# A two-layer kernel with a selective scan on one core: instruction order fixed in slots with three streams, and pairs of state products summed before their transpose

## The chip, the core and the metric

The kernel runs on one core of a Trainium2 chip. A core has TensorE (PE, matrix multiplies; its weight loads are shown apart as PEld), VectorE (DVE), ScalarE (ACT), GpSimd (POOL) and SyncE (SP, which here only issues DMAs). Each engine works through its own queue in order, and semaphores hold an instruction until its inputs are there and its buffer is free. The metric is device time in microseconds for one execution.

## What is computed

A sequence of 2048 rows of 512 float32 values goes through two layers. All arithmetic is float32.

```python
# layer 0
h = layernorm(x) * (1 + ca) + sa
x = x + ga * (h @ (block-masked W).T + bias)
h = layernorm(x) * (1 + cb) + sb
x = x + gb * lora_ffn(h)              # silu(gate) * up, hidden width 1376
# layer 1
h = layernorm(x) * (1 + ca) + sa
x, gate = split(h @ W_in.T)           # 1024 channels each
x = silu(causal_conv4(x))
ts, B, C = split(x @ W_x.T)           # 32, 16, 16 columns, each RMS-normed
dt = softplus(ts @ W_dt.T + b_dt)
for t in sequence:                    # 16 states n for each of 1024 channels
    state[n] = state[n] * exp(dt * A[n]) + dt * u * B[n]
    y = sum_n state[n] * C[n]
y = (y + x * D) * silu(gate)
x = x + ga * (y @ W_out.T)
h = layernorm(x) * (1 + cb) + sb
x = x + gb * (h @ base.T + 2 * top2_lora_experts(h))
```

The vectors sa, ca, ga and so on come from two small products with modulation weights, once for each layer.

## The kernel before

**Tiling.** The 2048 rows are cut into 8 chunks (`c`) of 256. The scan of a chunk runs in 32 steps: two halves of the channels (`a`, four tiles of 128 channels each) times 16 states (`n`). One such step is called a slot here; there are 256, and the loop over `ALL` makes them. Channels lie on the partitions, time along the free dimension, so a slot works on tiles of 128 x 1024 (four channel tiles of 256 time steps).

**One slot.** SP brings the rows B and C of state `n`, spread over all partitions (`bcn`, line 473). ACT makes the decays `da` two slots ahead (line 469). VectorE multiplies `bx = dtu * B` into PSUM (line 687), adds the carry of the chunk before into the first column of each tile (line 689) and runs the recurrence as one scan, `hb = scan(da, bx)` (line 690). ACT copies the last column out as the next carry (`states`, line 695). GpSimd multiplies `hc = hb * C` in two pieces of 128 x 512 (line 697). In the slot after, TensorE transposes the eight 128 x 128 blocks of `hc` and adds them in PSUM to `ys` (`add_t`, line 450): the sum over the 16 states is made there, by 16 x 8 transposes for each half. `da`, `hb` and `hc` have three buffers each, taken in turn; `bx` has one.

**Work beside the scan.** Everything else is written as generators, which issue a piece of work and yield its cost in us of TensorE time. `first_layer(c)` is layer 0 of a chunk: two norms with transposes (`norm_t`, lines 148 to 177), the masked product (line 286), gate and up projections (line 304) and the down projection (line 323). `beside(c)` holds, in this order, `out_proj(c-1)` (lines 509 to 525), `gate_proj(c)` (line 489), in the first chunk `late_setup` (scaled weights of layer 1), then `front(c+1)` (norm, input projection line 374, convolution line 394, B, C and dt rows lines 405 to 416) and `experts(c-1)` (lines 562 to 625). After the transposes of a slot the loop draws pieces worth 2.4 us from `beside` and 1.8 us from the first layers. At slot 10 of a second half it issues all that is left of `beside`; at slot 12 of each half it issues `steps` (dt, line 433) and `inputs` (`dtu`, line 439) of the next half.

**Order.** The order of writing is not the order on the engines. The tile framework's scheduler sorts the instructions of all engines by priority and by its own estimate of when each is ready, and places the waits.

**Buffers and queues.** Weights that don't stay in SBUF pass through 12 buffers `ws` of 256 KB, loaded on SP; temporaries have 5 buffers `tmp`; `bcn` has 6, fetched 4 slots ahead. PSUM has 4 banks for products, 2 for `ys`, 2 for `bx`. The weights of the experts' base product (`w_base`, 1 MB) stay in SBUF. `late_setup` loads its weights on ACT's queue.

**Before and after the loop.** The modulation, the masked weights, `first_layer(0)` and `front(0)` run ahead of the loop; the last `out_proj` and `experts` run behind it.

Of the kernel before, what the change touches and what calls it, by code (L numbers as in the profile page):

```python
# [23 lines left out]
R = 16  # L24
# [13 lines left out]
def mamba_block_kernel(  # L38
# [14 lines left out]
    small = ctx.enter_context(tc.tile_pool(name="small", bufs=2))  # L53
    xpool = ctx.enter_context(tc.tile_pool(name="x", bufs=5 * NM))
    wsp = ctx.enter_context(tc.tile_pool(name="ws", bufs=12))
    tpool = ctx.enter_context(tc.tile_pool(name="tmp", bufs=5))
    hpool = ctx.enter_context(tc.tile_pool(name="hT", bufs=1))
    hid = ctx.enter_context(tc.tile_pool(name="hid", bufs=6))
    upool = ctx.enter_context(tc.tile_pool(name="u", bufs=6))
    zpool = ctx.enter_context(tc.tile_pool(name="z", bufs=2 * NM))  # L60
    bcp = ctx.enter_context(tc.tile_pool(name="bc", bufs=6))
# [3 lines left out]
    ps_b = ctx.enter_context(tc.tile_pool(name="ps_b", bufs=1, space=PSUM))  # L65

# [22 lines left out]

    xs = {}  # L90
# [11 lines left out]
    da, hc = by_half("da", 3), by_half("hc", 3)  # L102
    hb_w = [keep.tile([P, FF], FP, name=f"hb{i}") for i in range(3)]
    hb = [t[:, : TH * TC].rearrange("p (t n) -> p t n", t=TH) for t in hb_w]
# [43 lines left out]
    def norm_t(xt, scale, shift, tag):  # L148
        st = small.tile([P, NM, 6], FP, tag="st", name="st")
        mv = small.tile([P, NM, 2], FP, tag="mv", name="mv")  # L150
        for m in range(NM):
            V.bn_stats(st[:, m, :], xt[m])  # L152
            V.bn_aggr(mv[:, m, :], st[:, m, :])  # L153
        rs = small.tile([P, NM], FP, tag="rs", name="rs")
        G.tensor_scalar(rs, mv[:, :, 1], LN_EPS, None, ALU.add)
        G.tensor_tensor(rs, rs, power, ALU.pow)
        off = small.tile([P, NM], FP, tag="off", name="off")
        V.scalar_tensor_tensor(off, mv[:, :, 0], -1.0, rs, ALU.mult, ALU.mult)
        xn = []
        for m in range(NM):  # L160
            t = tmp()
            S.activation(t, xt[m], AF.Identity, bias=off[:, m : m + 1], scale=rs[:, m : m + 1])  # L162
            xn.append(t)
        h = hpool.tile([P, NK, TC], FP, tag=tag, bufs=2 if tag == "h0" else 1, name="h")
        for k2 in range(NK // 2):
            ps = halves(bank())
            for i in range(2):
                k = 2 * k2 + i
                for m in range(NM):
                    T.transpose(ps[:, i, m * P : (m + 1) * P], xn[m][:, k * P : (k + 1) * P], ident)  # L170
            for i in range(2):
                k = 2 * k2 + i
                S.activation(  # L173
                    h[:, k, :], ps[:, i, :], AF.Identity, bias=shift[:, k : k + 1], scale=scale[:, k : k + 1]
                )
            yield 0.5
        return h
# [46 lines left out]
    ranks = [t.rearrange("p t n -> p (t n)")[:R, :DM] for t in hc]  # L224
    wides = [t[:R, :] for t in hb_w]
    for dst, src in zip(ranks + wides, (gate_a, up_a, down_bt, gate_bt, up_bt, down_a)):
        nc.gpsimd.dma_start(out=dst, in_=src)
    ga_r, ua_r, db_r = ranks
    gb_w, ub_w, da_w = wides
# [4 lines left out]
    down_s = dram.tile([len(HT), P, DM], FP, name="down_s")  # L234
    wout_s = dram.tile([ND, P, DM], FP, name="wout_s")

    def wide_tile(src, scratch, a_r, b_w, j, first):
# [8 lines left out]
        for k in range(NK):  # L246
            T.matmul(
                ps[:, k * n : (k + 1) * n], lhsT=a_r[:, k * P : (k + 1) * P], rhs=b_w[:, h0 : h0 + n],
                start=True, stop=True,
            )  # L250
# [4 lines left out]
    def down_tile(j, first):  # L255
# [8 lines left out]
        T.matmul(ps[:n, :], lhsT=da_w[:, h0 : h0 + n], rhs=db_r, start=True, stop=True)  # L264
# [5 lines left out]

    def first_layer(c):
        xt = xs[c]
        if c + 1 < NC:
            load(c + 1)
        h = yield from norm_t(xt, ca, sa, "h0")
        acc = [bank() for m in range(NM)]
# [13 lines left out]
        for m in range(NM):  # L290
            V.tensor_tensor(xt[m], xt[m], acc[m], ALU.add)
        h = yield from norm_t(xt, cb, sb, "h0")
        hidden = []
        product = None
        for j0 in range(0, len(HT), 2):
# [4 lines left out]
            pg, pu = halves(bank()), halves(bank())  # L300
            for w2, ps in ((ws_g, pg), (ws_u, pu)):
# [6 lines left out]
                yield 1.75 * len(js)  # L308
            ht = hid.tile([P, 2, TC], FP, tag="hid", name="hidden")
            up = halves(tmp())  # L310
            view = (slice(0, n), slice(0, len(js)))
            S.activation(ht[view], pg[view], AF.Silu)  # L312
            S.copy(up[view], pu[view])  # L313
            if product is not None:
                V.tensor_tensor(*product, ALU.mult)  # L315
            product = ht[view], ht[view], up[view]
            hidden.append(ht)
        V.tensor_tensor(*product, ALU.mult)
# [9 lines left out]
        for m in range(NM):  # L328
            V.tensor_tensor(xt[m], xt[m], acc[m], ALU.add)
        done.add(c)  # L330

    for _ in first_layer(0):
        pass
# [24 lines left out]
    def front(c):  # L358
        nonlocal halo
        h = yield from norm_t(xs[c], ca1, sa1, "h1")  # L360
        new_halo = keep.tile([P, ND, KC - 1], FP, name=f"halo{c % 2}", tag=f"halo{c % 2}")
        us = []
        for t2 in range(ND // 2):
            ps = halves(bank())
            xp = small.tile([P, 2, TC + KC - 1], FP, tag="xp", name="xp")
            for i in range(2):
# [6 lines left out]
                for k in range(NK):  # L373
# [3 lines left out]
                    )  # L377
                yield 1.75
            if halo is None:
                G.memset(xp[:, :, : KC - 1], 0.0)  # L380
            else:
                G.tensor_copy(xp[:, :, : KC - 1], halo[:, 2 * t2 : 2 * t2 + 2, :])
            S.copy(xp[:, :, KC - 1 :], ps)
            if c + 1 < NC:
                G.tensor_copy(new_halo[:, 2 * t2 : 2 * t2 + 2, :], xp[:, :, TC:])
            acc = halves(tmp())
            for i in range(2):
                t = 2 * t2 + i
                S.activation(  # L389
                    acc[:, i, :], xp[:, i, KC - 1 :], AF.Identity,  # L390
                    bias=ch[:, t, C_B : C_B + 1], scale=ch[:, t, C_W + KC - 1 : C_W + KC],
                )
                for j in range(KC - 1):
                    V.scalar_tensor_tensor(  # L394
                        acc[:, i, :], xp[:, i, j : j + TC], ch[:, t, C_W + j : C_W + j + 1],
                        acc[:, i, :], ALU.mult, ALU.add,
                    )
            u = upool.tile([P, 2, TC], FP, tag="u", name="u")
            S.activation(u, acc, AF.Silu)
            us.append(u)  # L400
        halo = new_halo

# [5 lines left out]
        yield 3.5  # L408
        sq = tmp()
        S.activation(sq[:64, :TC], ps[:64, :TC], AF.Square)  # L410
        ps2 = bank()
        T.matmul(ps2[:64, :TC], lhsT=rms_m, rhs=sq[:64, :TC], start=True, stop=True)
        S.activation(sq[:64, TC:], ps2[:64, :TC], AF.Sqrt, bias=eps_rms[:64, :])
        V.reciprocal(sq[:64, :TC], sq[:64, TC:])
# [3 lines left out]
        nc.sync.dma_start(out=bc.rearrange("a n t -> (a n) t"), in_=ssm[RDT:, :])  # L418
        fed[c] = (h, us, ssm, bc)
        yield 0.5  # L420

    bx = ps_b.tile([P, TH, TC], FP, name="bx")

    def steps(c, a):
        us, ssm = fed[c][1:3]
        for i in range(TH):
            t = a * TH + i
            ps = bank()
            T.matmul(
                ps[:, :TC], lhsT=wdt[:, t * P : (t + 1) * P], rhs=ssm[:RDT, :], start=True, stop=True  # L430
            )
            dst, src, b_dt = dt[a][:, i, :], ps[:, :TC], ch[:, t, C_DT : C_DT + 1]
            S.activation(dst, src, AF.Softplus, bias=b_dt)  # L433
# [21 lines left out]
    def skip(c, a):  # L455
        us = fed[c][1]
        for t2 in range(TH // 2):
            ud = halves(tmp())
# [21 lines left out]
    def gate_proj(c):  # L480
        h = fed[c][0]
        zs[c] = [zpool.tile([P, DM], FP, tag="z", name="z") for _ in range(2 * NM)]
        for a in range(2):
            acc = [bank() for m in range(NM)]
# [8 lines left out]
            for m in range(NM):  # L493
                S.activation(zs[c][2 * m + a], acc[m], AF.Silu)

    def gating(c, a):
        for m in range(NM):
            z = zs[c][2 * m + a]
            V.tensor_tensor(z, z, ys[m], ALU.mult)

    def out_proj(c):
        xt = xs[c]
        acc = [bank() for m in range(NM)]
        for t2 in range(ND // 2):
            ps = halves(bank())
# [7 lines left out]
            g = halves(tmp())  # L513
            S.copy(g, ps)  # L514
            for i in range(2):
                t = 2 * t2 + i
                w = ws()
                nc.sync.dma_start(out=w, in_=wout_s[t])
                for m in range(NM):
                    T.matmul(  # L520
                        acc[m], lhsT=g[:, i, m * P : (m + 1) * P], rhs=w, start=t == 0, stop=t == ND - 1
                    )
                yield 2.0
        for m in range(NM):
            V.tensor_tensor(xt[m], xt[m], acc[m], ALU.add)  # L525
# [270 lines left out]
```

## Time and profile before

| What | Value |
|---|---|
| median of three runs | 1911.51 us (1905.35 to 1913.41) |
| the profiled execution, its own time | 1914.97 us |
| span of its trace (first to last instruction) | 1913.2 us |
| first scan starts, last one ends (the loop) | 242.8 us, 1869.8 us |
| mean granted TensorE clock | 0.881 |
| ACT busy | 1003.0 us (52%) |
| GpSimd busy | 879.3 us (46%) |
| DMA traffic | 233.42 MB, 122 GB/s over the span |

The trace is of one execution. Its page lists the busy time of each engine, and then groups of equal instructions with their count, busy time, mean duration, and the idle time of their engine just before them with what ended it. Busy time of TensorE is modelled: neighbouring matmuls overlap, so a busy TensorE is not one at its peak. The granted clock is the share of full speed that TensorE was allowed in a stretch. The durations of GpSimd contain the time in which an instruction has begun but is held up.

### The profile page before, as it was taken

The numbers are of one execution on the slowest core, as the hardware profiler recorded it, in microseconds if no ns is written. First come the engines' busy times: TensorE is split into PE (matmuls) and PEld (weight loads), VectorE is DVE, ScalarE is ACT, GpSimd is POOL, SyncE is SP. The second block draws the span as 40 slices with busy tenths as digits, with TensorE's granted clock in tenths as the row PEclk, the third lists the DMA queues.
The fourth block names the chain that finished last, engine by engine and source line by source line (L and its number), as shares of the span: only waits on it lengthen the run. The fifth ranks groups of instructions, "written<-read, shape, count | busy, mean of one in ns | idle before, by whom it ended". The sixth has DMA issues, their size and how long they took to land. (4 is left out here: it accounts for less than half of the span.)

```text
span 1913.2 us, 20659 instructions
## 1 busy us (share of the span) xinstructions
PE 1577.2 (82%) x6568; PEld 1075.1 (56%) x6568; DVE 1385.8 (72%) x1563; ACT 1003.0 (52%) x2093; POOL 879.3 (46%) x721
## 2 busy tenths in 40 slices
PE   4899779878897689879888879878888979767666
PEld 4685648545565466556546645555546655644433
DVE  2222395796877877887878886897678896989992
ACT  0100463557655565666565665575466765565631
POOL 0133072463553454544544554455344555547671
PEclk9689779988998899989898989898898989878877
DMA  8454345563554245534464345433353345423320
GB/s 248 147 159 165 102 124 172 149 192 99 143 149 104 85 125 151 128 100 122 130 153 103 95 114 142 118 98 119 115 149 110 95 124 147 121 51 98 72 51 11
DMA packets 192367, 233.42 MB, mean 122 GB/s; under 512 B 17009, under 2 KB 128497, under 8 KB 192258
## 3 DMA queue, kind: packets, MB, share of 16 engines
q1 hardware_dynamic: 176800, 200.13, 38.6%
q10 hardware_dynamic: 10434, 15.81, 2.5%
q0 software_dynamic: 5024, 16.16, 2.3%
q8 instruction: 52, 0.85, 0.2%
q14 instruction: 57, 0.47, 0.1%
HBM read 215.99 MB, written 16.06 MB: 121 GB/s over the span
## 5 line engine op out<-in xcount | busy, mean ns | idle before, releaser
L697 POOL TENSOR_TENSOR hc<-hb,bcn 128x512 f32<-128x512 f32 x512 | 777.1, 1538 | 642.1 <-PE y L450 469.7
L690 DVE TENSOR_TENSOR_SCAN hb<-da,bx 128x1024 f32<-128x1024 f32 x256 | 584.7, 2284 | 117.4 <-POOL hc L697 91.9
L469 ACT ACTIVATE da<-dt,neg_a 128x255 f32<-128x255 f32 x1024 | 440.9, 497 | 65.3 <-DVE hb L690 48.7
L304 PE MATMUL ps<-h,ws 128*128 128x256 f32 (+1 forms) x1408 | 344.6, 400 | 26.5 <-ACT hidden L312 18.3
L687 DVE TENSOR_TENSOR bx<-dtu,bcn 128x1024 f32<-128x1024 f32 x256 | 356.2, 1392 | 11.3 <-DMA bcn<-bc 5.0
L450 PE MATMUL y<-ident,hc 128*128 128x128 f32 x2048 | 303.2, 293 | 49.7 <-POOL hc L697 49.0
L304 PEld LDWEIGHTS ps<-h,ws 128*128 128x128 f32 (+1 forms) x1408 | 276.2, 200 | 99.2 <-issue 22.1
L450 PEld LDWEIGHTS y<-ident,hc 128*128 128x128 f32 x2048 | 256.1, 151 | 134.3 <-POOL hc L697 73.3
L695 ACT COPY states<-hb 128x4 f32<-128x4 f32 x224 | 43.5, 196 | 367.5 <-DVE hb L690 353.8
L520 PE MATMUL ps<-ws,tmp 128*128 128x512 f32 x256 | 151.8, 739 | 63.4 <-ACT tmp L514 63.3
L323 PE MATMUL ps<-ws,hidden 128*128 128x512 f32 (+1 forms) x352 | 161.6, 599 | 0.8 <-DVE ws L265 0.8
L394 DVE SCALAR_TENSOR_TENSOR tmp<-xp,ch,tmp 128x256 f32<-128x256 f32 x192 | 115.5, 649 | 19.9 <-ACT tmp L389 19.1
L520 PEld LDWEIGHTS ps<-ws,tmp 128*128 128x128 f32 x256 | 57.2, 238 | 129.5 <-ACT tmp L514 70.5
L374 PE MATMUL ps<-h,ws 128*128 128x256 f32 x512 | 125.1, 395 | 0.7 <-ACT h L173 0.7
L489 PE MATMUL ps<-ws,h 128*128 128x512 f32 x256 | 120.5, 602 | 2.6 <-ACT hidden L312 2.6
L374 PEld LDWEIGHTS ps<-h,ws 128*128 128x128 f32 x512 | 98.8, 200 | 16.5 <-ACT h L173 3.8
L323 PEld LDWEIGHTS ps<-ws,hidden 128*128 128x128 f32 (+1 forms) x352 | 64.0, 192 | 69.8 <-issue 63.1
L315 DVE TENSOR_TENSOR hidden<-hidden,tmp 128x512 f32<-128x512 f32 x40 | 38.9, 971 | 81.1 <-ACT tmp L313 81.1
L170 PE MATMUL ps<-ident,tmp 128*128 128x128 f32 x256 | 51.8, 343 | 52.6 <-ACT tmp L162 52.6
L162 ACT ACTIVATE tmp<-x,off,rs 128x512 f32<-128x512 f32 x64 | 48.9, 806 | 87.8 <-DVE mv L153 46.0
L469 ACT ACT_TABLE_LOAD x71 | 91.1, 1283 | 1.1
L170 PEld LDWEIGHTS ps<-ident,tmp 128*128 128x128 f32 x256 | 39.5, 178 | 72.6 <-ACT tmp L162 60.9
(140 smaller groups left out, 1575.7 us busy)
## 6 DMA issues: line engine op xcount, KB each, us to landing
bcn<-bc SPq DMA_DIRECT2D x256, 256.0 KB, 5.1
ws<-gate_s SPq DMA_DIRECT2D x70, 256.0 KB, 4.6
ws<-up_s SPq DMA_DIRECT2D x70, 256.0 KB, 4.7
ws<-down_s SPq DMA_DIRECT2D x70, 256.0 KB, 5.2
ws<-win_x_t_dram SPq DMA_DIRECT2D x64, 256.0 KB, 5.7
ws<-win_z_t_dram SPq DMA_DIRECT2D x64, 256.0 KB, 3.2
ws<-wout_s SPq DMA_DIRECT2D x64, 256.0 KB, 4.3
ws<-wmod_dram ACTq DMA_DIRECT2D x36, 256.0 KB, 3.2
```

The costliest lines, as they stand in the source:

```text
L170: T.transpose(ps[:, i, m * P : (m + 1) * P], xn[m][:, k * P : (k + 1) * P], ident)
L304: T.matmul(ps[:n, i, :], lhsT=w3[:, k, :], rhs=h[:, k, :], stop=k == NK - 1, **start_only(4 * i + k),)
L323: T.matmul(acc[m], lhsT=hidden[j // 2][:n, j % 2, m * P : (m + 1) * P], rhs=w[:n, :], start=j == 0, stop=j == len(HT) - 1,)
L374: T.matmul(ps[:, i, :], lhsT=w3[:, k, :], rhs=h[:, k, :], stop=k == NK - 1, **start_only(4 * i + k),)
L394: V.scalar_tensor_tensor(acc[:, i, :], xp[:, i, j : j + TC], ch[:, t, C_W + j : C_W + j + 1], acc[:, i, :], ALU.mult, ALU.add,)
L450: T.matmul(ys[m][:, i * P : (i + 1) * P], lhsT=src[:, m * P : (m + 1) * P], rhs=ident, start=first and i == 0, stop=last, is_transpose=Tru ...
L469: S.activation(da[q % 3][:, i, 1:], dt[a][:, i, 1:], AF.Exp, scale=neg_a[:, t, n : n + 1])
L489: T.matmul(acc[m], lhsT=h[:, k, m * P : (m + 1) * P], rhs=w, start=k == 0, stop=k == NK - 1)
L520: T.matmul(acc[m], lhsT=g[:, i, m * P : (m + 1) * P], rhs=w, start=t == 0, stop=t == ND - 1)
L687: V.tensor_tensor(bx, dtu[a], bcn[:, 0:1, :].to_broadcast([P, TH, TC]), ALU.mult)
L690: V.tensor_tensor_scan(h.rearrange("p t n -> p (t n)"), d.rearrange("p t n -> p (t n)"), bx.rearrange("p t n -> p (t n)"), 0.0, ALU.mult, ...
L697: G.tensor_tensor(hcn[:, i : i + 2, :], h[:, i : i + 2, :], bcn[:, 1:2, :].to_broadcast([P, 2, TC]), ALU.mult)
```

## The change

1. **Fixed order.** From the loop on, the order of writing is the order on PE, DVE, ACT and GpSimd (`manual_schedule`); SP is left to the framework. The writer keeps a clock of its own (`tick`), in us of TensorE work. An evacuation, an activation or a VectorE step that follows a product is written when that clock has moved on by a stated delay (`later`), and generators yield `WAIT` times.
2. **Three streams.** The first layers, `beside` (now with `steps` and `inputs` of both halves in it) and `experts` are three streams with shares 1.8, 2.0 and 0.4. A slot draws 2.3 us of work twice (4.0 us twice in the first half of chunk 0, where the first layers have share 6.0). A stream is passed over while it waits, while its PSUM banks or temporaries are taken (`NEED`), or while another stream holds the pair of accumulating banks (`HOLD`, `FREE`). The forced completion at slot 10 goes. First layers may run up to two chunks ahead of the scan.
3. **Pairs.** `hc` has four buffers. In an even slot, between the two draws, VectorE adds the `hc` of the two slots before, `due[0] += due[1]`, 128 x 1024 in SBUF; in the odd slot after it, TensorE transposes the sum: 8 transposes for two states in place of 16.
4. **Small moves.** The norm's `off` goes from VectorE to two GpSimd instructions; the halo copies of the convolution go from GpSimd to ACT; the copy of `states` is written 3.0 us later; `late_setup` loads on SP; the base weights of the experts are scaled once, written to DRAM (`base_s`) and loaded again in each chunk through `ws`, and their product follows the choice of the experts; `out_proj` makes all its transposes ahead of its products; `steps` puts two products in a bank. Three DMAs more split the wide rank weights ahead of the first layer. `ws` has 11 buffers, `tmp` 7, `bcn` 5 (fetched 3 slots ahead); `ud`, `g` and the norm's columns have pools of their own.

The loop afterwards, and the code around it that sets the order:

```diff
-    da, hc = by_half("da", 3), by_half("hc", 3)
+    da, hb, hc = by_half("da", 3), by_half("hb", 3), by_half("hc", 4)
...
         G.tensor_scalar(rs, mv[:, :, 1], LN_EPS, None, ALU.add)
+        G.tensor_scalar(off, mv[:, :, 0], -1.0, None, ALU.mult)
         G.tensor_tensor(rs, rs, power, ALU.pow)
-        V.scalar_tensor_tensor(off, mv[:, :, 0], -1.0, rs, ALU.mult, ALU.mult)
+        G.tensor_tensor(off, off, rs, ALU.mult)
+        yield WAIT, 5.0
+        yield NEED, 0, NM
...
+    def pump(streams, budget):
+        total = sum(st.share for st in streams if not st.ended) or 1.0
+        for st in streams:
+            if not st.ended:
+                st.credit = min(st.credit + budget * st.share / total, 12.0)
+        while budget > 0:
+            best = max((st for st in streams if ready(st)), key=lambda st: st.credit, default=None)
+            if best is None:
+                tick(min(budget, 0.5))
+                budget -= 0.5
+            else:
+                budget -= step(best)
+        return budget
...
     def beside(c):
+        yield from steps(c, 1)
         if c > 0:
             yield from out_proj(c - 1)
         yield from gate_proj(c)
...
             yield from front(c + 1)
-        if c > 0:
-            yield from experts(c - 1)
+            yield from steps(c + 1, 0)
...
     for q, (c, a, n) in enumerate(ALL):
...
+        first.share = 1.8 if c > 0 or a == 1 else 6.0
+        streams = [first, second, third]
+        budget = 2.3 if c > 0 or a == 1 else 4.0
+        while q + AHEAD < len(ALL) and ALL[q + AHEAD][:2] not in stepped:
+            pump(streams, 0.5)
+        h, d, hcn, bcn = hb[q % 3], da[q % 3], hc[q % 4], bcs.pop(0)
...
-        if n == NS - 6 and a == 1:
-            while not finished:
-                cost = next(second, "end")
...
-        if n == NS - 4 and nxt[0] < NC:
-            steps(*nxt)
-            inputs(*nxt)
         if q + 2 < len(ALL):
             decays(q + 2)
         V.tensor_tensor(bx, dtu[a], bcn[:, 0:1, :].to_broadcast([P, TH, TC]), ALU.mult)
...
         for i in range(0, TH, 2):
             G.tensor_tensor(
                 hcn[:, i : i + 2, :], h[:, i : i + 2, :], bcn[:, 1:2, :].to_broadcast([P, 2, TC]), ALU.mult
             )
+        if c + 1 < NC:
+            later(3.0, lambda a=a, n=n, h=h: S.copy(states[a][:, :, n], h[:, :, TC - 1]))
+        over = pump(streams, over + budget)
+        if n == 2 and q > NS:
+            gating(*ALL[q - 3][:2])
+        if n == 3:
             skip(c, a)
-        if due is not None:
+        due.append((hcn, n))
+        if n % 2 == 0 and len(due) > 2:
+            V.tensor_tensor(due[0][0], due[0][0], due[1][0], ALU.add)
+        if n % 2 == 1 and len(due) > 2:
+            src, at = due[0][0], due[1][1]
+            due = due[2:]
             for i in range(TH):
-                add_t(i, due[:, i, :], False, n == 0)
-        due = hcn
...
+                add_t(i, src[:, i, :], False, at == NS - 1)
+            tick(1.1)
+        over = pump(streams, over + budget)
```

## Prediction

> **What bounds the kernel now.** I read the busy line of the page first, then the loop by stretches, then who waits for whom, then single slots.
>
> ```profile
> PE 1577.2 (82%) x6568; PEld 1075.1 (56%) x6568; DVE 1385.8 (72%) x1563; ACT 1003.0 (52%) x2093; POOL 879.3 (46%) x721
> ```
>
> No engine is full. TensorE comes first, but its 82% is modelled time. The starts of neighbouring matmuls in the trace lie 0.109 us apart for a 128-column transpose, 0.216 for 256 columns and 0.43 for 512 (medians). By these the loop's matmuls need 1196 us at full clock, and 1196/0.89 = 1344 at the clock granted there, of a loop of 1627. The stretches (columns: us, then PE, PEld, DVE, ACT, POOL busy with counts, clock, DMA share, GB/s) are the whole loop, two halves of chunk 3, and the two halves of chunk 7:
>
> ```profile
> 242.80:1869.80 1627.00, 1346.19 (x5714) 911.65 (x5713) 1312.29 (x1407) 953.93 (x2007) 831.81 (x636) 0.89 0.43 118
> 892.60:983.60 91.00, 77.64 (x318) 50.23 (x317) 72.62 (x61) 57.90 (x125) 49.25 (x32) 0.92 0.50 132
> 983.60:1101.00 117.40, 99.17 (x445) 70.53 (x444) 98.34 (x129) 70.61 (x148) 53.91 (x51) 0.90 0.41 110
> 1724.90:1798.60 73.70, 59.58 (x248) 37.22 (x249) 69.20 (x67) 45.87 (x96) 53.83 (x34) 0.86 0.39 100
> 1798.60:1869.80 71.20, 40.70 (x170) 24.10 (x168) 68.85 (x65) 28.05 (x68) 50.35 (x32) 0.75 0.21 45
> ```
>
> VectorE is busy 1312 of 1627 us, so it idles 315. Where the side work runs out (chunk 7) it is busy 94% and 97%: there it is the bound. In the chunks before, VectorE and TensorE wait for each other in turn:
>
> ```profile
> POOL hc L697 <- PE y L450: 469.7, 132, 19.3
> DVE hb L690 <- POOL hc L697: 91.9, 39, 7.2
> DVE hidden L315 <- ACT tmp L313: 81.1, 19, 9.7
> DVE dtu L439 <- ACT dt L433: 58.4, 19, 6.0
> ```
>
> The first two are one chain: late transposes keep `hc`, so GpSimd is late, keeps `hb`, and the scan waits. The others are work issued in lumps, before its inputs are there.
>
> **The pair sum: what it takes away.** 2048 transposes of `hc` become 1024: 1024 x 0.109 = 112 us of TensorE, 125 at clock 0.89. TensorE's need falls from 1344 to 1219 us, far below VectorE's. So I count this gain as nothing by itself; it makes TensorE punctual, which works through the idle time below.
>
> **What it adds.** 128 adds of 128 x 1024 on VectorE, both inputs in SBUF. No such instruction is in the trace; the nearest is `bx`, also 128 x 1024 from two SBUF tiles, which goes to PSUM: shortest 1199 ns, median 1233. An instruction starts some 80 ns before its neighbour ends, so I take 1.15 us: 128 x 1.15 = 147 us.
>
> The price is not only that. In slot 1172 to 1181 and in a run of six convolution steps GpSimd and VectorE overlap:
>
> ```profile
> 1177.35 3.48 POOL L697 TENSOR_TENSOR hc<-hb,bcn 128x512 f32<-128x512 f32 x2 [2.30 <-PE y L450]
> 1177.40 2.30 DVE L687 TENSOR_TENSOR bx<-dtu,bcn 128x1024 f32<-128x1024 f32 x1
> ...
> 428.70 4.47 DVE L394 SCALAR_TENSOR_TENSOR tmp<-xp,ch,tmp 128x256 f32<-128x256 f32 x6
> 428.92 2.78 POOL L697 TENSOR_TENSOR hc<-hb,bcn 128x512 f32<-128x512 f32 x2 [0.57 <-PE ps L170]
> ```
>
> `bx` takes 2.30 instead of 1.23 because one `hc` piece (1.27 median) began first; six steps of 0.47 take 4.47 because two pieces slip in between, each after the step that held it up. The scan, whose `bx` is in PSUM, never moves (2244 to 2289 ns), nor does gating with `y` in PSUM (660 to 687). So VectorE instructions with both inputs in SBUF and GpSimd's `hc` exclude each other. The new add stands just where GpSimd has `hc` of the scan before it to do: if the add begins right after the scan, the first piece follows it and the next `bx` waits for that piece; if a stream's step comes first, the add itself waits.
>
> Call the wait per add b. Below: 0, the lone `bx` (no gain is possible, since the add only takes the tiles). Above: two pieces, 2 x 1.27 = 2.5; that can't hold for most adds, since the second piece falls under the next scan, which lets it run, so one piece, 1.27, is the end that I carry into the range. `bx` shows 1392 - 1233 = 0.16 on average, `dtu` (both in SBUF, not placed behind a scan, 665 shortest, 1168 mean in the loop) 0.50, a full block 1.13 (`dtu`'s longest, 1802, less 665). I take 0.8, halfway from `dtu` to the full block, because of the place: 128 x 0.8 = 102 us.
>
> The Trainium skill, "SBUF — State Buffer", section "Who interferes with whom", says that a VectorE instruction with two SBUF inputs and a GpSimd instruction that reads SBUF lock each other out for the whole instruction, whoever issues first. It speaks against the change more strongly than my 0.8: a whole piece for each add would be 128 x 1.27 = 163 us in place of 102, and the forecast 65 us later.
>
> **Norm.** `off` leaves VectorE: 27 x 0.46 = 12 us in the loop. GpSimd gets two small instructions more for each norm (0.3 us, as line 155) behind `hc`; it is 51% busy, and `off` was waited for 24.3 us in all, now inside a stated 5 us wait. Gain 12 us.
>
> **The order.** The loop's VectorE sum becomes 1312 - 12 + 147 + 102 = 1549 us. What idle time stays? The forced completion, `steps` and `inputs` in a lump, and `hc` freed late go. By the writer's clock a chunk offers 32 x 4.6 + 16 x 1.1 = 165 us and its side work is 134 (69 first layer, 53 `beside`, 12 experts), so the streams fit without overrun. TensorE has slack, ACT (954 of 1627) too. I take the 6% of chunk 7's first half, which still carries `out_proj` and `gate_proj`: 1549/0.94 = 1648. Bounds: 3% (the last half) gives 1597, 10% gives 1721.
>
> **Chunk 0.** Its first half now offers 16 x 8.0 + 8 x 0.87 = 135 us of TensorE work at full clock, 153 at 0.88, against 105.7 us for that half and 84 us of such work in it before. VectorE needs there only 71 + 8 x 1.95 = 87, 95 to 100 with the front brought forward. TensorE is the bound for some 50 us; part returns, since work brought forward (up to 51 us of TensorE, some 10 us of VectorE, and an emptier second half) is missing later. I charge 30; from 0 (the streams wait too, and idle ticks pass quickly) to 50.
>
> **The small moves.** Halo copies: 52 x 0.2 = 10 us to ACT, hidden by its slack; uncovered they would add at most these 10. Table loads (139 in the loop, 1.28 each) may rise when activations of three streams mix; ten more per chunk are 100 us, making ACT 1060 of 1650: hidden too. Base weights: 32 loads of 256 KB, 8.4 of 233 MB at a DMA share of 0.43: hidden; the row for such loads shows 8.0 us of waits (`ws` of `attn_s`, 128 products), so 8 uncovered. `late_setup` on SP passes the `bcn` loads: VectorE waited 5.0 us for `bcn` in all, ACT 5.5 behind its own weight loads; these trade, 0, from -5 to +21 (the longest wait for such a weight). Prefetch of `bcn` (6 less 4 slots, now 5 less 3) is tied to the same `hc` two slots back: 0. The three DMAs on POOL at the start cost some 0.6 us each beside a TensorE that is full there: 0.
>
> At the end, `experts` now makes the base product after the choice. Before, its 7.34 us ran from 1894.97 beside VectorE's 3.7 us of choosing. Now it starts after the transposes: 4 us.
>
> **Sum.** Loop 1648 + 30 - 1627 = +51, end +4: 1914.97 + 55 = 1970 for an execution like the profiled one, which is 3.5 over the median. Forecast 1966 us.
>
> **Rivals.** Each loop below becomes a time by + 30 (chunk 0) + 4 (end) + 288 (1914.97 less the loop of 1627) - 3.5. *Locks are light, order smooth.* The adds land in gaps, b = 0.16 as for `bx` now, 4% idle: (1312 - 12 + 147 + 20)/0.96 = 1528: 1846. For it: `hc` can run under the scan, which it never disturbs (2.3 us for 2.5 us of pieces). Against: in a slot with an add the lock is wanted three times between two scans. It decides below b = 0.4: there 1300 + 147 + 51 = 1498 at 6% idle is 1594, and with 30 + 4 the old loop of 1627.
> *Locks fall everywhere.* VectorE's instructions at their tenth percentile make 1219 in place of 1363 in the loop; (both sums of durations); if a steadier order takes 100 of these 144 us away and adds are free, (1312 - 12 - 100 + 147)/0.95 = 1418: 1736.
> *Adds fit the idle time.* VectorE idles 315 us and the added 249 go in; in-order waits keep the pace: 1911.
> *Full lock.* b = 1.27 and 8% idle, since every wait in an order that can't adapt holds all behind it: 1610/0.92 = 1750: 2068. For it: the 1177 row. Against: pieces can finish under the scan.
> That the change doesn't do what it says is small: the transposes are halved by count; only the streams could fail to mix, if `HOLD` serialises them, and that ends in the last case.
>
> **Numbers.** Forecast 0.40 (own range 1925 to 2015), light locks 0.24, falling locks 0.06, fit 0.10, full lock 0.20. Half a per cent, 10 us, is about what a measurement can tell from no change. Faster: 0.24 + 0.06 + 0.03 of the fit = 0.33. Same: 0.05 of the fit and 0.02 of the forecast's edge = 0.07. Slower 0.60. The range 1830 to 2065 leaves out the falling locks, the low end of the light ones and the upper half of the full lock.
>
> **What would show it.** Right: VectorE over 90% busy in the loop, the add at 1.7 to 2.2 us mean or `bx` risen from 1392, `hc`'s waits for line 450 nearly gone, first half of chunk 0 over 130 us, the other halves nearer to each other than 91 and 117. Wrong: VectorE below 85% (in-order waits), adds at 1.25 with `bx` unchanged (light locks), or convolution and `dtu` rows at their shortest (locks fall).

## The result, and the profile after

The changed kernel takes 1982.98 us (median of four runs, 1981.06 to 1988.66) against 1908.43 for the kernel before: ratio 1.0397, 95% interval 1.0356 to 1.0438. It is slower, as forecast, and 17 us over the forecast of 1966. The profiled execution took 1981.06 us, 66 more than the one profiled before.

The page of the changed kernel, its busy line and three of its groups (line, engine, operation, tiles, shapes, count, then busy us and mean ns, then idle time before them):

```profile
PE 1479.9 (75%) x5544; PEld 983.9 (50%) x5544; DVE 1616.3 (82%) x1659; ACT 1041.3 (53%) x2173; POOL 1018.4 (51%) x736
...
L926 POOL TENSOR_TENSOR hc<-hb,bcn 128x512 f32<-128x512 f32 x512 | 901.0, 1779 | 707.4 <-issue 312.3
...
L918 DVE TENSOR_TENSOR bx<-dtu,bcn 128x1024 f32<-128x1024 f32 x256 | 431.4, 1685 | 3.6 <-DMA bcn<-bc 1.6
...
L938 DVE TENSOR_TENSOR hc<-hc,hc 128x1024 f32<-128x1024 f32 x127 | 165.2, 1301 | 0.1
```

VectorE is now the busier of the two, before it was TensorE. The sum itself (L938) costs 1301 ns, little over the 1205 ns that it takes in a run below where GpSimd is out of the way. What has grown is `bx`, from 1392 to 1685 ns, and GpSimd's `hc`, whose recorded mean rose from 1538 to 1779 ns for the same 128 x 512 elements. Stretches of the loop (columns as before: us, PE, PEld, DVE, ACT, POOL, clock, DMA share, GB/s): the whole loop, the two halves of chunk 0, two of chunk 3, two of chunk 7, and what follows the loop:

```profile
231.00:1921.90 1690.90, 1253.00 (x4672) 824.97 (x4670) 1542.88 (x1511) 993.83 (x2087) 969.56 (x648) 0.84 0.44 120
231.00:373.20 142.20, 122.29 (x447) 82.25 (x446) 94.32 (x90) 73.75 (x144) 63.28 (x59) 0.86 0.63 184
373.20:487.10 113.90, 93.76 (x378) 70.85 (x377) 101.93 (x85) 81.48 (x163) 60.26 (x37) 0.86 0.44 114
912.80:1010.50 97.70, 77.07 (x256) 41.21 (x256) 93.00 (x94) 53.97 (x123) 59.44 (x37) 0.90 0.45 119
1010.50:1123.40 112.90, 70.35 (x297) 52.31 (x296) 102.63 (x106) 73.30 (x150) 61.58 (x47) 0.79 0.38 108
1748.20:1843.20 95.00, 56.81 (x195) 33.20 (x196) 90.92 (x90) 46.84 (x98) 59.21 (x37) 0.76 0.35 92
1843.20:1921.90 78.70, 18.16 (x76) 13.68 (x74) 76.02 (x58) 23.84 (x57) 60.25 (x34) 0.55 0.23 58
1921.90:1979.30 57.40, 35.26 (x102) 20.07 (x102) 10.35 (x33) 6.82 (x14) 4.99 (x8) 0.77 0.04 14
```

VectorE is busy 1543 of 1691 us, 91%; before it was 1312 of 1627, 81%. Only in the first half of chunk 0 is it far from full: there it is busy 94 of 142. The loop grew by 64 us, the stretch behind it by 14 (57.4 against 43.4), and the one ahead of it is 12 shorter.

The waits in the changed kernel (who waited for whom, us in total, times, longest):

```profile
PE y L581 <- DVE hc L938: 174.2, 40, 12.8
...
DVE hidden L345 <- ACT tmp L393: 75.8, 16, 9.0
...
DVE dtu L570 <- ACT dt L549: 21.2, 11, 3.3
```

GpSimd's 470 us of waiting for transposes are gone from the list, and so are the scan's 92 for `hc`; TensorE now waits for VectorE's sum. GpSimd does not idle less for it: it idles 707 us before `hc` where it was 642, now 302 of them for the scan, and for 312 (`issue`) the profile shows no cause. One slot with a sum, on VectorE and GpSimd:

```profile
1360.93 2.29 DVE L921 TENSOR_TENSOR_SCAN hb<-da,bx 128x1024 f32<-128x1024 f32 x1
1363.13 1.20 DVE L938 TENSOR_TENSOR hc<-hc,hc 128x1024 f32<-128x1024 f32 x1
...
1363.45 4.22 POOL L926 TENSOR_TENSOR hc<-hb,bcn 128x512 f32<-128x512 f32 x2 [1.63 <-DVE hb L921]
...
1364.25 2.31 DVE L918 TENSOR_TENSOR bx<-dtu,bcn 128x1024 f32<-128x1024 f32 x1
```

The sum begins straight after the scan and takes its 1.20 us. GpSimd's first piece has begun at 1363.45, waits, and goes next. `bx` begins at 1364.25, 0.08 us before the sum has ended, and needs 2.31 us in place of 1.23: it waits for that piece. The second piece is recorded as ending at 1367.67, under the next scan.

This slot is typical. Of the 96 `bx` that follow a sum directly on VectorE, 87 took over 2 us; of the 160 others, 21. And in the whole trace, where a piece that had begun before `bx` was still unfinished, 112 of 118 `bx` took over 1.4 us; of the 138 others none did.

### The profile page after: what moved, and what is told of

Read it like the earlier page. It is cut to its first block, busy times and chain, and to the rows that moved or that the text cites. A ratio compares the mean times of both kernels' runs of the same rounds, so it can differ in the third digit from the quotient of the medians.

```text
span 1979.3 us, 18729 instructions
## 1 busy us (share of the span) xinstructions
PE 1479.9 (75%) x5544; PEld 983.9 (50%) x5544; DVE 1616.3 (82%) x1659; ACT 1041.3 (53%) x2173; POOL 1018.4 (51%) x736
## 4 chain that ended last, share of the span: by engine, by line
DVE 46%; PE 30%; issue 10%; DMA 6%; ACT 6%; POOL 2%; SPq 0%; DVEq 0%; POOLq 0%
DVE bx L918 13%; DVE hb L921 12%; PE ps L400 7%; DVE hc L938 5%; PE ps L418 5%; DVE tmp L486 5%; PE ps L668 3%; PE y L581 2%; PE ps L627 2%; PE ps L168 2%; ACT da L600 1%; DVE bx L920 1%; DVE st L198 1%; DVE x L341 1%; PE ps L557 1%
## 5 line engine op out<-in xcount | busy, mean ns | idle before, releaser
L926 POOL TENSOR_TENSOR hc<-hb,bcn 128x512 f32<-128x512 f32 x512 | 901.0, 1779 | 707.4 <-issue 312.3
L918 DVE TENSOR_TENSOR bx<-dtu,bcn 128x1024 f32<-128x1024 f32 x256 | 431.4, 1685 | 3.6 <-DMA bcn<-bc 1.6
L581 PE MATMUL y<-ident,hc 128*128 128x128 f32 x1024 | 163.2, 312 | 180.9 <-DVE hc L938 174.2
L581 PEld LDWEIGHTS y<-ident,hc 128*128 128x128 f32 x1024 | 139.2, 162 | 225.9 <-DVE hc L938 197.6
L418 PE MATMUL ps<-ws,hidden 128*128 128x512 f32 (+1 forms) x352 | 176.5, 654 | 6.9 <-DMA ws<-down_s 4.9
L938 DVE TENSOR_TENSOR hc<-hc,hc 128x1024 f32<-128x1024 f32 x127 | 165.2, 1301 | 0.1
L486 DVE SCALAR_TENSOR_TENSOR tmp<-xp,ch,tmp 128x256 f32<-128x256 f32 x192 | 126.0, 676 | 19.2 <-ACT tmp L472 14.9
L668 PE MATMUL ps<-ws,g 128*128 128x512 f32 x256 | 113.6, 596 | 0.0
L345 DVE TENSOR_TENSOR hidden<-hidden,tmp 128x512 f32<-128x512 f32 (+1 forms) x48 | 34.9, 726 | 75.8 <-ACT tmp L393 75.8
L341 DVE TENSOR_TENSOR x<-x,ps 128x512 f32<-128x512 f32 x64 | 41.4, 677 | 55.0 <-PE ps L668 17.9
```

The costliest lines, as they stand in the source:

```text
L418: T.matmul(acc[m], lhsT=hidden[j // 2][:n, j % 2, m * P : (m + 1) * P], rhs=w[:n, :], start=j == 0, stop=j == len(HT) - 1,)
L486: V.scalar_tensor_tensor(acc[:, i, :], xp[:, i, j : j + TC], ch[:, t, C_W + j : C_W + j + 1], acc[:, i, :], ALU.mult, ALU.add,)
L581: T.matmul(ys[m][:, i * P : (i + 1) * P], lhsT=src[:, m * P : (m + 1) * P], rhs=ident, start=first and i == 0, stop=last, is_transpose=Tru ...
L668: T.matmul(acc[m], lhsT=gs[t // 2][:, t % 2, m * P : (m + 1) * P], rhs=w, start=t == 0, stop=t == ND - 1,)
L918: V.tensor_tensor(bx, dtu[a], bcn[:, 0:1, :].to_broadcast([P, TH, TC]), ALU.mult)
L926: G.tensor_tensor(hcn[:, i : i + 2, :], h[:, i : i + 2, :], bcn[:, 1:2, :].to_broadcast([P, 2, TC]), ALU.mult)
```

## Experiments

The theory: VectorE is the bound; the sums cost it their own time and a wait for one GpSimd piece each, and the transposes saved on TensorE are worth nothing. The main rival: the fixed in-order streams cost the time, and the sums fit into idle time.

**order_only.** The changed kernel without the sums. The small moves and the fourth `hc` stay.

```diff
-        if n % 2 == 0 and len(due) > 2:
-            V.tensor_tensor(due[0][0], due[0][0], due[1][0], ALU.add)
-        if n % 2 == 1 and len(due) > 2:
-            src, at = due[0][0], due[1][1]
-            due = due[2:]
+        if len(due) > 2:
+            src, at = due.pop(0)
...
```

> The changed kernel with the fixed order and all small moves, but without the pair sums: each state's product is transposed by itself, two slots later. Theory (VectorE is the bound, the sums and their waits cost more than the order gains): VectorE's loop of 1543 us loses 127 x 1.22 = 155 for the sums and some 75 as bx falls from 1685 to about 1.4 us, so 1310; TensorE needs again 1196 at full clock, 1375 at 0.87. The loop ends between 1480 and 1600, the time between 1770 and 1890, below the kernel before. Rival (the fixed in-order streams themselves cost the time, the sums fit in idle time): 1950 or more.

Measured: 1882.53 us, ratio 0.9867 (0.9846 to 0.9888). Its loop, and its `bx`:

```profile
235.40:1823.90 1588.50, 1326.83 (x5693) 917.87 (x5692) 1291.33 (x1384) 992.40 (x2090) 875.36 (x648) 0.89 0.47 128
```

```profile
L918 DVE TENSOR_TENSOR bx<-dtu,bcn 128x1024 f32<-128x1024 f32 x256 | 334.7, 1307 | 5.5 <-DMA bcn<-bc 1.0
```

This lies inside the expected range, at its upper end. The fixed order with the small moves is 1.3% faster than the kernel before, so the rival falls; what each of these two parts gives was not separated. The sums cost 100 us on top. Without them VectorE has 252 us less work (1543 to 1291), but it idles 297 us where it was 148: it is no longer the bound everywhere.

**pairs_only.** The kernel before, in the framework's order, with the sums.

```diff
-    da, hc = by_half("da", 3), by_half("hc", 3)
+    da, hc = by_half("da", 3), by_half("hc", 4)
...
+        if n % 2 == 0 and len(due) > 2:
+            V.tensor_tensor(due[0][0], due[0][0], due[1][0], ALU.add)
...
```

The lines left out transpose the sum in the odd slot, as in the changed kernel.

> The kernel before, with its order left to the framework, plus only the pair sums (and a fourth hc buffer). Theory: VectorE's 1312 us gain 155 for the sums and some 75 in waits of bx, 1540; part of the 315 idle us is used up since TensorE is relieved. Loop 1660 to 1740, time 1945 to 2030. Rival (the order costs, sums are nearly free): 1925 or less, since TensorE loses 112 us of need.

Measured: 2062.75 us, ratio 1.0794 (1.0762 to 1.0826), above the range, and by another mechanism than expected. Loop, `bx` and sum, and the longest wait of VectorE:

```profile
229.40:2005.10 1775.70, 1289.64 (x4694) 822.07 (x4692) 1460.88 (x1534) 990.82 (x2038) 894.28 (x636) 0.83 0.41 108
```

```profile
L687 DVE TENSOR_TENSOR bx<-dtu,bcn 128x1024 f32<-128x1024 f32 x256 | 360.6, 1409 | 5.3
L706 DVE TENSOR_TENSOR hc<-hc,hc 128x1024 f32<-128x1024 f32 x127 | 157.9, 1243 | 170.3 <-POOL hc L697 170.3
```

`bx` hardly moved. In this order the sum comes up on VectorE before GpSimd has made the second product, and waits for it outright: 170 us. VectorE's busy time rose by 149 us, about the sums alone, and its idle time stayed at 315. So the sums are dear in either order, and they are 80 us cheaper in the kernel with the fixed order and the small moves. Why the framework's order leaves as much idle time as before is open.

The four kernels side by side, by the loop, VectorE's busy time in it and its idle time, in us:

| | framework's order | fixed order, small moves |
|---|---|---|
| each product transposed by itself | 1627, 1312, 315 | 1588, 1291, 297 |
| pair sums | 1776, 1461, 315 | 1691, 1543, 148 |

**pieces_256 and piece_1024.** GpSimd's product in pieces of another size; nothing else changes. The two comments say which run has the line.

```diff
-        for i in range(0, TH, 2):
-            G.tensor_tensor(
-                hcn[:, i : i + 2, :], h[:, i : i + 2, :], bcn[:, 1:2, :].to_broadcast([P, 2, TC]), ALU.mult
-            )
+        for i in range(TH):                                   # pieces_256
+            G.tensor_tensor(hcn[:, i, :], h[:, i, :], bcn[:, 1, :], ALU.mult)
+        G.tensor_tensor(hcn, h, bcn[:, 1:2, :].to_broadcast([P, TH, TC]), ALU.mult)   # piece_1024
```

> The changed kernel with GpSimd's product in four pieces of 128x256 in place of two of 128x512. Theory (one piece that is ready slips between the sum and the next bx, which waits until it has ended): the wait falls from about 1.1 to 0.6 us, bx from 1685 to some 1450 ns on average, the time by 30 to 80 us, to 1900 to 1955. Rival (bx is longer for other reasons, such as traffic in general, or VectorE's own work alone sets the time): bx within 50 ns of 1685 and the time within 15 us of 1983, or above it by the dispatch of 512 more instructions.

> The changed kernel with GpSimd's product in one piece of 128x1024. Theory: a wait lasts up to the whole piece, 2.4 us: bx over 2.0 us on average, time 2040 to 2150. Rival (bx longer for other reasons): bx near 1685, time within 20 us of 1983.

Measured: 1930.2 us in four pieces (ratio 1.0097, 1.0071 to 1.0123), 1982.98 in two, 2079.41 in one (a single run), each inside its range. The two groups in the run with four pieces, and with one:

```profile
L918 DVE TENSOR_TENSOR bx<-dtu,bcn 128x1024 f32<-128x1024 f32 x256 | 371.9, 1453 | 3.1 <-DMA bcn<-bc 1.1
L936 DVE TENSOR_TENSOR hc<-hc,hc 128x1024 f32<-128x1024 f32 x127 | 164.4, 1295 | 4.0 <-POOL hc L926 0.6
```

```profile
L918 DVE TENSOR_TENSOR bx<-dtu,bcn 128x1024 f32<-128x1024 f32 x256 | 512.7, 2003 | 3.2 <-DMA bcn<-bc 1.1
L935 DVE TENSOR_TENSOR hc<-hc,hc 128x1024 f32<-128x1024 f32 x127 | 183.8, 1447 | 0.0
```

`bx` goes 1453, 1685, 2003 ns with the piece, though GpSimd's total work, at its shortest durations, is greatest with small pieces (4 x 0.71 against 2 x 1.25 us a slot). What VectorE waits for is the one piece that slips in between. The longest `bx` is 1.77, 2.32 and 3.41 us, that is 1.23 and one piece, 0.71, 1.25 or 2.34 (the shortest of each kernel), less some 0.17. This agrees with the Trainium skill, "SBUF — State Buffer", section "Who interferes with whom", by which whoever issues first keeps the shared port pair for its whole instruction and the other is blocked until then.

**pool_8cols.** The product with C is cut to 8 of 256 columns of each tile; the rest of it is left out. Sums and transposes stay.

```diff
-                hcn[:, i : i + 2, :], h[:, i : i + 2, :], bcn[:, 1:2, :].to_broadcast([P, 2, TC]), ALU.mult
+                hcn[:, i : i + 2, :8], h[:, i : i + 2, :8], bcn[:, 1:2, :8].to_broadcast([P, 2, 8]), ALU.mult
...
```

A line left out here clears the `hc` tiles once, ahead of the loop.

> The changed kernel with GpSimd's product cut to the first 8 of 256 columns of each tile: the rest of the product with C is left out. The sums on VectorE and all transposes stay. Theory (the waits for GpSimd's pieces are what makes the sums dear): bx and the sum fall to 1.23 and 1.20 us, VectorE's sum of durations to some 1390, the loop to 1440 to 1540, time 1730 to 1830. Rival (the sums' own 150 us and the order set the time, not the waits): 1900 or more.

Measured: 1800.15 us (a single run), inside the range; its loop, and the two groups:

```profile
230.60:1742.90 1512.30, 1203.74 (x4672) 796.45 (x4670) 1335.80 (x1511) 989.38 (x2088) 395.74 (x648) 0.88 0.50 134
```

```profile
L920 DVE TENSOR_TENSOR bx<-dtu,bcn 128x1024 f32<-128x1024 f32 x256 | 315.9, 1234 | 3.2 <-DMA bcn<-bc 1.2
L940 DVE TENSOR_TENSOR hc<-hc,hc 128x1024 f32<-128x1024 f32 x127 | 153.0, 1205 | 0.0
```

With GpSimd out of the way `bx` and the sum take their lone times, the loop 1512 us, VectorE 1336 of it. All waits of VectorE for GpSimd in the changed kernel, not only those that the sums bring, are thus worth 1543 - 1336 = 207 us of its busy time.

**sum_16.** The sums stay, but TensorE makes 16 transposes a pair again: eight of the sum, eight of a tile of zeros.

```diff
-                add_t(i, src[:, i, :], False, at == NS - 1)
-            tick(1.1)
+                add_t(i, src[:, i, :], False, False)
+            for i in range(TH):
+                add_t(i, zero, False, at == NS - 1)
+            tick(2.2)
...
```

The line left out makes the tile of zeros.

> The changed kernel, with the pair sums, but TensorE makes 16 transposes for each pair as before: eight of the sum and eight of a tile of zeros, which add nothing. The writer's clock counts them. Theory (VectorE is the bound, so the 1024 transposes that the sums save TensorE, 112 us at full clock, are worth nothing by themselves): bx and the sum as in the changed kernel, within 60 ns; time 1980 to 2010. Rival (the sums pay part of their price back through TensorE): 2025 or more.

Measured: 1983.5 us against 1982.98, ratio to before 1.0406 (1.0358 to 1.0455). The stretch of the changed kernel's loop, `bx` and the sum:

```profile
231.00:1921.90 1690.90, 1330.91 (x5688) 927.18 (x5686) 1539.96 (x1511) 993.85 (x2088) 964.35 (x648) 0.87 0.44 120
```

```profile
L920 DVE TENSOR_TENSOR bx<-dtu,bcn 128x1024 f32<-128x1024 f32 x256 | 426.5, 1666 | 3.4 <-DMA bcn<-bc 1.4
L940 DVE TENSOR_TENSOR hc<-hc,hc 128x1024 f32<-128x1024 f32 x127 | 159.2, 1254 | 0.2
```

The transposes that the change saves are worth nothing once the sums are there. The run also settles another rival. The granted clock in the loop fell from 0.89 to 0.84 with the change, and one could blame it for the time. Here it is 0.87, with more work on TensorE, and the time is the same.

**ends.** Two places of the changed kernel that the forecast had priced by themselves.

```diff
...
-        first.share = 1.8 if c > 0 or a == 1 else 6.0
+        first.share = 1.8 if c > 0 or a == 1 else 4.0
...
-        budget = 2.3 if c > 0 or a == 1 else 4.0
+        budget = 2.3 if c > 0 or a == 1 else 3.0
...
+        if c == NC - 1 and a == 1 and (fourth or second.ended and third.ended):
+            fourth = fourth or Stream(out_proj_last(c), 1.0)
+            streams.append(fourth)
...
-    run(out_proj(NC - 1))
+    finish([fourth], fourth)
...
+        if c == NC - 1:      # experts: the base product ahead of the choice
...
```

The cut gives the lines out of their order in the file, and its comment stands for the product that follows. `out_proj_last` transposes, copies and multiplies tile pair by tile pair, as before the change.

> The changed kernel with two places altered. In the first half of chunk 0 a slot draws 3.0 us of work twice in place of 4.0, the first layers having share 4.0; and at the end the last out_proj takes its first four channel tiles as a stream of their own while the last half scans, and the last base product is issued ahead of the choice of experts, as in the kernel before. Theory (chunk 0 is bound by the TensorE work that it is given, the end by work that was no longer brought forward): the first half of chunk 0 falls from 142 to about 118 us, of which 5 to 10 come back later; the stretch behind the loop falls from 57 to 43 to 48; time 1945 to 1965. Rival (both are only shares of work that has to be done anyway): 1975 or more.

Measured: 1944.15 us, ratio 1.0179 (1.0141 to 1.0217), 1 us below the range. The first half of chunk 0 and what follows the loop:

```profile
235.10:353.80 118.70, 100.17 (x393) 69.94 (x392) 97.25 (x78) 73.41 (x143) 63.57 (x52) 0.88 0.60 177
1894.30:1942.00 47.70, 27.78 (x78) 15.21 (x78) 10.33 (x32) 5.74 (x12) 4.99 (x8) 0.75 0.03 11
```

142 became 119 and 57 became 48; the loop is 32 us shorter in all (1659), so nothing came back later.

**single_ends and single_ends_256.** Both edits together: no sums, and the two places altered; then GpSimd's four pieces on top.

> The fixed order without the pair sums (each product transposed by itself) and with the two places altered as in the run before this one. If the gains add up: 1882 less 15 to 35, that is 1845 to 1870, and both kernels are beaten by over 2%. If TensorE, which is the fuller one here (1190 us at full clock), sets the time of chunk 0 anyway: 1870 to 1885.

> The run before this one with GpSimd's product in four pieces of 128x256. Theory: without the sums bx waits little (1307 ns on average), and all waits for GpSimd in VectorE's sum are some 90 us, which shorter pieces can halve; since VectorE is not the bound everywhere, the time falls by 5 to 30 us. Rival (GpSimd's longer total, 4 x 0.72 in place of 2 x 1.27 us a slot, makes hc late): the same or slower.

Measured: 1822.31 us, ratio 0.9552 (0.9519 to 0.9585), better than expected and below both kernels; and 1821.47, ratio 0.9526 (0.949 to 0.9561), which can't be told from it, so the 5 to 30 us expected of the small pieces are not there. The loop of the first:

```profile
233.20:1770.70 1537.50, 1315.51 (x5717) 907.24 (x5716) 1290.18 (x1384) 982.47 (x2082) 878.29 (x648) 0.90 0.50 132
```

VectorE is busy 84% and TensorE's modelled share is 86%: neither is full. Here small pieces shorten VectorE's work by 21 us (1269) without shortening the loop by more than 3 us (1535): VectorE's work is not what sets it.

## Why the prediction was right, step by step

- **The bound.** VectorE over 90% busy: 91%. Its sum was forecast as 1549 us and is 1543.
- **TensorE's saving counted as nothing.** `sum_16` shows it: 1983.5 with and 1983.0 without the 1024 extra transposes.
- **The sums' own time**, 147 us: 127 x 1.205 (the lone duration in `pool_8cols`) is 153, less the overlap of some 0.08 each, 143 in the loop.
- **The wait, b = 0.8, 102 us.** Over their lone durations `bx` and the sum now wait (1685 - 1234) x 256 + (1301 - 1205) x 127 = 128 us, against 40 of `bx` before: 88 more, b = 0.69. The forecast had also said which instruction would wait, and the slot at 1363, the 87 of 96 `bx` behind a sum and the piece sizes show it. Not each add costs a whole piece, which would be the 163 us of the full lock.
- **Idle time, 6%.** Outside the first half of chunk 0 VectorE idles 100 of 1549 us, 6.5%. The number is right, the reason given for it only in part. The forecast put it down to the order, which would clear away the lumps and the late `hc`. But `order_only` has that order and idles 297 of 1588 us, 19%, as the kernel before (315 of 1627). The idle time falls only where the order and the sums come together: VectorE's 252 us of added work made the loop 102 us longer, the rest took the place of idle time. In the framework's order they took none of it.
- **Chunk 0, 30 us.** Forecast 153 us for its first half, measured 142; easing it took 32 us off the loop. Right in size for what could be had back, but VectorE idles 48 us there. This is where the loop's excess lies: the forecast was 1549 + 99 (the 6%) + 30 = 1678, and the loop is 1543 + 100 + 48 = 1691.
- **The end, 4 us: mis-sized.** It cost 14. The late base product was seen. Overlooked was the last `out_proj`: before, the framework had moved its first half into the last scans (16 products, 8.22 us together, stood behind the loop), and the fixed order writes all 32 behind it (13.9 us). `ends` gives 10 us back.
- **Ahead of the loop, 0.** The changed kernel entered the loop 12 us earlier. This is not its doing: `pairs_only`, with the older code there, entered at 229.4, and `pieces_256`, with the newer code, at 241.1. It goes with the granted clock of the execution: the mean ahead of the first scan is 0.83 in the kernel before and 0.82 in `pieces_256`, and 0.87 in the changed kernel and in `pairs_only`. Clock times length is about 200 us in all four. Why the clock differed is not known.
- **Small moves.** The norm's `off` is gone from VectorE. Table loads in the loop rose from 162 (the forecast's 139 was a miscount) to 186, 31 us of ACT at 1.28, hidden as assumed; `bcn` makes `bx` wait 1.6 us in all.

The parts add up to 64 - 12 + 14 = 66 us where 55 were forecast. That they come so near is partly luck: the 12 us ahead of the loop, which are not the change's, hide half of what the loop (13) and the end (10) were forecast too low. By the medians, 1982.98 against 1908.43, the change costs 75 us.

The forecast gave no price for the order without the sums. With the small moves it is a gain of 27 us, hidden under the sums, and 60 more that the crowded first half of chunk 0 and the end take away (1882.53 to 1822.31).

## What to carry to other kernels

A step that moves work from one engine to another must be priced on the engine that will be full afterwards, and there with its neighbours: an instruction of 1.2 us cost 1.9, mostly because GpSimd's next piece went between it and its successor. Where two engines exclude each other and one of them is the bound, the size of the other's pieces is part of the price: cutting them in half took 53 us off the kernel with the sums, and nothing that could be measured off the one without. A low idle share can also come from the added work itself, not from a better order. And a change of several parts is best taken apart: the order with its small moves was worth keeping, the sums were not.

## What the runs showed of the hardware

A VectorE instruction with two SBUF inputs and GpSimd's `hc` run one after the other, as a rule in the order in which they began. In the slot at 1363 the piece began at 1363.45 and `bx` at 1364.25, both while the sum ran, and the piece went first. So a VectorE instruction that follows another at once can lose one piece: 87 of the 96 `bx` behind a sum did. The recorded duration of a piece includes its own wait (in the changed kernel 1.25 us at the shortest, 2.26 at the ninetieth percentile).

The kernel before has one exception, in its longest `bx` (shortest, median and longest in ns):

```profile
L687 DVE TENSOR_TENSOR bx<-dtu,bcn x256: 1199/1233/7034, 241.4 to 1865.9; 128x1024 f32<-128x1024 f32 x128
```

It began at 1825.09, beside a piece that had begun before it, and took 7.03 us. Four more pieces, which began at 1825.50, 1827.31, 1828.53 and 1829.76, ran ahead of it at 1.26 to 1.27 us each, with an issue of a DMA by GpSimd after the first of them. What kept `bx` back so long is open.
